# Attention of a four-layer graph network: weighted values by quarters of the queries, one order for every step

## The chip, the cores and the metric

The kernel runs on one core of one Trainium2 chip. The metric is the device time of one execution in microseconds (us). Three runs of the kernel before took 13,794.12, 13,808.5 and 13,815.49 us; the median is 13,808.5 us.

## The reference

Sixteen graphs of 1024 nodes with 64 features go through four layers. Each layer adds its result to its input and normalises. The change lies in layer 1, attention with 8 heads, which for each graph computes:

```
qkv   = x @ W_qkv.T                       # 8 heads of 64
attn  = (q @ k.T) / 8                     # per head, 1024 x 1024
attn  = g0 * attn + g1 * adj              # g0, g1 = exp(x @ W_gamma.T + b), per query node
out   = softmax(attn) @ v                 # per head, 1024 x 64
x     = layernorm(x + concat(out) @ W_proj.T + b_proj)
```

Layer 0 is a normalised graph convolution. Layer 2 takes quantiles of every feature over each node's neighbours, which the kernel finds from a sort of the features (`sort`) and a search over words of bits (`quantiles`). Layer 3 is a second graph convolution. All of them are left as they are, except for one buffer count in the sort.

## The kernel before

Graphs go in pairs. A loop of nine rounds does, in round p, layer 0 for pair p, then the attention of pair p with the sort of pair p-1 beside it, then the quantiles of pair p-1; layers 2 and 3 of a pair end in the round after. So there are eight stages of attention, each with both graphs of a pair, and a ninth sort that has no attention beside it.

One attention stage has 64 steps: 2 graphs x 4 pairs of heads (`hp`) x 2 halves of the queries (`nh`) x 4 blocks of 128 queries (`k4`). I call four steps with the same `nh` a half. A step has three pieces of work on TensorE, and this document uses short names for them:

- **Scores** (`scores`, L509): query times key for two heads, 128 queries x 1024 keys each, into two PSUM tiles called `banks` of two banks each; there are two such tiles, so four banks. VectorE then adds the adjacency and finds the row's extreme in one custom instruction per head (L516), which also frees the PSUM tile, and ScalarE takes the exponential (L518) with the row sum.
- **Transposes** (`transposes`, L529): the 2 x 8 blocks of the exponentials are transposed by TensorE, four into each of four PSUM tiles called `bank` (one bank each). ScalarE copies each of the four into the SBUF tile `pT` (L531). The pool `ps1` holds just four such `bank` tiles, and everything else that TensorE writes in the attention, projections (L488), values (L500), weighted values (L537) and output heads (L552), takes its tiles from the same four.
- **Weighted values** (`weighted`, L537): once per half, after its fourth step, 32 matmul instructions of 512 columns (8 blocks of keys x 2 heads x 2 passes for float32) sum into one `bank` tile `po`, which ScalarE copies into `o` (L540).

The order of TensorE's instructions in a stage is written out by hand: `in_sequence` gives a function `then` that ties every matmul to the one before it. A step issues the scores of the *next* step, then its own transposes. In the fourth step of a half the scores of the step after next are issued too, ahead of the weighted values. Projections of the next pair of heads follow the transposes in the steps (nh, k4) = (0, 2) and (1, 0). Values of a graph are made in its first four steps; the output heads of graph 0 in the first four steps of graph 1.

The order on VectorE and ScalarE is not written by hand. The tile framework lays each engine's queue out when the kernel is built, from its own estimate of when operands are ready, with the order of the program as priority. The sort's VectorE instructions (L1082) are emitted in step 58 (`BESIDE`) and so have low priority and fill gaps; `PACE` ties each swap of its second part to a score instruction that it may not overtake: 3, 9, 3 and 2 swaps for four steps in turn, the 9 falling on a step with weighted values. Its masks go to DRAM and come back through SP's queue, in tiles of which there are five.

Of the kernel before, what the change touches and what calls it, by code (L numbers as in the profile page):

```python
# [3 lines left out]

# [9 lines left out]
F32 = mybir.dt.float32  # L14
F16 = mybir.dt.float16
# [10 lines left out]
P = 128  # L26
N = 1024
C = 64
H = 8
NB = N // P  # L30
# [18 lines left out]
BESIDE = 58  # L49
AHEAD = (10, 12, 15)  # L50
STEPS = 55
PACE = (3, 9, 3, 2)
BN_EPS = 1e-5
LN_EPS = 1e-5

# [55 lines left out]
def gnn_kernel(ctx: ExitStack, tc: tile.TileContext, a: dict, out: bass.AP):  # L111
    nc = tc.nc
# [99 lines left out]
    def bank(shape, dtype=F32):  # L212
        return ps1.tile(shape, dtype, name="bank")
# [30 lines left out]
    HALF = [slice(0, C), slice(C, P)]  # L244
# [226 lines left out]
    def attention(nat, ip, graphs, wqkv, x2, beside):  # L471
# [3 lines left out]
        pace = []  # L475
        with (tc.tile_pool(name="att", bufs=2, reuse_waits="tile") as att,
# [3 lines left out]
            then = in_sequence()  # L480
# [12 lines left out]
            def values(gr, k):  # L493

                if k == 0:
                    gr.v = att1.tile([P, NB, H * C], F32, name="v")
                    gr.o = [att1.tile([P, N], F32, name=f"o{hp}") for hp in range(H // 2)]
                ps = [bank([P, H * C]) for f in range(2)]
                for f in range(2):
                    then(nc.tensor.matmul(ps[f], gr.xT[HALF[f], k * P:(k + 1) * P], wqkv[HALF[f], 2 * H * C:],  # L500
                                          start=True, stop=True))
                for f in range(2):
                    nc.scalar.copy(gr.v[:, 4 * f + k, :], ps[f])
# [17 lines left out]
                pace.append(last)  # L521
                return exps

            def transposes(exps, pT, k4):
                for h in range(2):
                    for mh in range(2):
                        ps = bank([P, 4, P])
                        for m in range(4):
                            then(nc.tensor.transpose(  # L529
                                ps[:, m, :], exps[h][:, (4 * mh + m) * P:(4 * mh + m + 1) * P], ident))  # L530
                        nc.scalar.copy(pT[h][mh][:, :, k4 * P:(k4 + 1) * P], ps)  # L531

            def weighted(gr, hp, nh, pT):
                po = bank([P, 512])
                for m in range(NB):
                    for h in range(2):
                        then(nc.tensor.matmul(po[HALF[h]], gr.v[:, m, (2 * hp + h) * C:(2 * hp + h + 1) * C],  # L537
                                              pT[h][m // 4][:, m % 4, :], start=(m == 0),
                                              stop=(m == NB - 1), tile_position=(0, h * C)))
                nc.scalar.copy(gr.o[hp][:, nh * 512:(nh + 1) * 512], po)  # L540

            def heads(gr, k):

                if k == 0:
                    nc.vector.reciprocal(gr.sm, gr.sm)
                smv = gr.sm.rearrange("p (f k) (q h) -> p h k f q", f=2, h=2)
                t = att1.tile([P, 2, 2, 4, C], F32, name="t_pr")
                pr = [bank([P, 2, 4, C]) for h in range(2)]
                for f in range(2):
                    for hp in range(H // 2):  # L550
                        for h in range(2):
                            then(nc.tensor.matmul(pr[h][:, f, hp, :],  # L552
                                                  gr.o[hp][HALF[h], (4 * f + k) * P:(4 * f + k + 1) * P],
                                                  wp[HALF[h], hp, :], start=True, stop=True))
                for h in range(2):
                    nc.vector.tensor_tensor(t[:, :, h], pr[h],
                                            smv[:, h, k, :, :, None].to_broadcast([P, 2, 4, C]), ALU.mult)
                x = gr.xg[:, k]
                nc.vector.tensor_reduce(x, t.rearrange("p f h q c -> p f c (h q)"), AX.X, ALU.add)
                nc.vector.tensor_tensor(x, x, bp_r[:, None, :].to_broadcast([P, 2, C]), ALU.add)  # L560
                nc.vector.tensor_tensor(x, x, gr.x1[:, k], ALU.add)
                if k == 0:
                    gr.norm = norm_tiles()
                norm_stats(gr.norm, gr.xg, [k])
                if k == 3:
                    norm_apply(gr.norm, by_half(x2)[:, :, :, gr.bb, :], gr.xg)
# [10 lines left out]
            def scores_of(st):  # L577
                if st < len(steps) and st not in exps:
                    gr, hp, nh, k4 = steps[st]
                    exps[st] = scores(gr, hp, 4 * nh + k4)  # L580

            scores_of(0)
            for st, (gr, hp, nh, k4) in enumerate(steps):
                if k4 == 0:
                    pT = [[att1.tile([P, 4, 512], F32, name="pT", bufs=4) for mh in range(2)] for h in range(2)]
                scores_of(st + 1)
                transposes(exps.pop(st), pT, k4)
                if k4 == 3:
                    scores_of(st + 2)
                at = 8 * hp + 4 * nh + k4  # L590
                if at < 4:
                    if gr is g1:
                        heads(g0, at)
                    values(gr, at)
                if st == BESIDE:
                    beside(pace)
                if st in AHEAD:
                    (keys_of, gates, queries_of)[AHEAD.index(st)](g1, att1, then)
                if gr is g0 and hp == H // 2 - 1:

                    k = 4 * nh + k4
                    g1.adj[k] = nat.tile([P, N], F32, name=f"adj{k}")
                    (nc.sync if k % 2 else nc.scalar).dma_start(
                        g1.adj[k], adj2d[ds((2 * ip + 1) * N + k * P, P), :])
                    gated(g1, k)
                if (nh, k4) in ((0, 2), (1, 0)):
                    if hp + 1 < H // 2:
                        project(gr, hp + 1, nh)
                    elif gr is g0:
                        project(g1, 0, nh)  # L610
                if k4 == 3:
                    weighted(gr, hp, nh, pT)
            for k in range(4):
                heads(g1, k)
            nc.gpsimd.dma_start(x2_d[ds(ip * P, P)], x2)
# [457 lines left out]
    def sort(keys, pool, key, pace, rk, u_w, b_w):  # L1073

        v = nc.vector

        behind = chain([None] * (3 * STEPS), (p for p, n in zip(pace, cycle(PACE)) for _ in range(n)))

        def swap(*args):
            i = v.tensor_tensor(*args)  # L1082
            p = next(behind, None)
            if p is not None:
                tc.add_manual_dep(i.ins, p.ins.name, in_order, reason="pace of the sort")


        steps = [(size, h) for p in range(1, 11) for size in (2 ** p,)
                 for h in [0] + [size >> s for s in range(2, p + 1)]]

        def pair(x, size, h):
            if h:
                r = x.rearrange("p (n two h) -> p n two h", two=2, h=h)
                return r[:, :, 0, :], r[:, :, 1, :]
            r = x.rearrange("p (n two h) -> p n two h", two=2, h=size // 2)
            return r[:, :, 0, :], r[:, :, 1, ::-1]

        def shaped(x, size, h):
            return x.rearrange("p (n h) -> p n h", h=h or size // 2)

        assert len(steps) == STEPS
        for i, (size, h) in enumerate(steps):
            new = keys.tile([P, N], F32, name="key", bufs=2)
            lo, hi = pair(key, size, h)
            nlo, nhi = pair(new, size, h)
            mask = keys.tile([P, N // 2], F16, name="mask", bufs=5)
            swap(shaped(mask, size, h), lo, hi, ALU.is_gt)
            nc.sync.dma_start(masks_d[:, i, :], mask)
            swap(nlo, lo, hi, ALU.min)
            swap(nhi, lo, hi, ALU.max)  # L1110
            key = new

        rank = pool.tile([P, N], F16, name="rank")
        nc.sync.dma_start(rank, a["c_iota"])
        d = pool.tile([P, N // 2], F16, name="d")
        for i, (size, h) in reversed(list(enumerate(steps))):
            lo, hi = pair(rank, size, h)
            mask = keys.tile([P, N // 2], F16, name="mask", bufs=5)
            nc.sync.dma_start(mask, masks_d[:, i, :])
            ds = shaped(d, size, h)  # L1120
            swap(ds, hi, lo, ALU.subtract)
            swap(ds, ds, shaped(mask, size, h), ALU.mult)
            swap(lo, lo, ds, ALU.add)
            swap(hi, hi, ds, ALU.subtract)
        words_of(pool, rank, rk, u_w, b_w)
        return key
# [110 lines left out]
```

## Time and profile before

The profiled execution took 13,812.89 us, 4.4 us more than the median of the three; its span, from the first to the last instruction in the profile, is 13,811.1 us. All numbers below are from this execution.

| What | us |
|---|---|
| TensorE busy, whole span | 12,369.8 (90%) |
| VectorE busy, whole span | 10,477.1 (76%) |
| ScalarE busy, whole span | 7,462.0 (54%) |
| Eight attention stages, first score to last weighted value, summed | 3,678.3 |
| One typical stage (5903.3 to 6362.0) | 458.7 |
| TensorE, ScalarE, VectorE busy in that stage | 437.8, 312.9, 276.4 |
| Granted TensorE clock in that stage, share of full | 0.97 |

A matmul's time in the profile is modelled and matmuls overlap in the array, so "busy" doesn't mean that the array is at its limit. What a group of matmuls really takes is read from the start of its first instruction to the start of the next group. In the timeline, "x16" after an instruction means that so many were merged into one row, and the brackets give the idle time of the engine before it and what ended that wait. In the chain, each row is the piece of time that the last instruction of the window had to wait for, followed backwards.

### The profile page before, as it was taken

How to read it: one execution, taken by the hardware profiler on the slowest of the kernel's cores; microseconds unless marked ns; L12 is line 12 of the kernel's file. 1: busy time of each engine (PE TensorE's matmuls, PEld its weight loads, DVE VectorE, ACT ScalarE, POOL GpSimd, SP SyncE). 2: the span in 40 equal slices, each digit the busy share in tenths (PEclk: the TensorE clock that was granted, in tenths of full speed). 3: DMA queues.
4: the chain of work that ended last, by engine and by line, in shares of the span. 5: the costliest groups of instructions: out<-in, count | busy, mean ns of one | idle time of the engine just before them, and what ended most of it. 6: DMA issues, size and time to landing. Idle time of an engine off the chain costs nothing.

```text
span 13811.1 us, 207433 instructions
## 1 busy us (share of the span) xinstructions
PE 12369.8 (90%) x81455; PEld 5244.9 (38%) x81536; DVE 10477.1 (76%) x18187; ACT 7462.0 (54%) x13548; POOL 635.5 (5%) x948
## 2 busy tenths in 40 slices
PE   7889998899979899798997989979899798993998
PEld 3544333443325433254333533335333353331332
DVE  3486887668876688766987678866788667887895
ACT  5666554555546555365553655536555465551553
POOL 0000000000000000000000000000000001000000
PEclk9999998999989999899998999989999899996999
DMA  2120002100031000310003100031000300002001
GB/s 76 34 92 21 4 6 94 63 17 4 5 104 53 16 5 5 119 40 14 5 5 128 32 13 6 5 130 30 14 5 5 131 29 14 9 8 88 4 5 43
DMA packets 356342, 510.35 MB, mean 37 GB/s; under 512 B 124448, under 2 KB 279584, under 8 KB 353312
## 3 DMA queue, kind: packets, MB, share of 16 engines
q1 hardware_dynamic: 288656, 371.94, 8.4%
q10 hardware_dynamic: 34192, 87.14, 2.0%
q0 software_dynamic: 32512, 38.00, 1.0%
q8 instruction: 638, 10.45, 0.3%
q14 instruction: 344, 2.82, 0.1%
HBM read 380.32 MB, written 116.59 MB: 36 GB/s over the span
## 4 chain that ended last, share of the span: by engine, by line
PE 68%; DVE 14%; ACT 6%; DMA 4%; issue 2%; SPq 0%; ACTq 0%; DVEq 0%
PE bank L815 33%; PE acc L815 9%; PE bank L537 6%; PE banks L509 6%; PE bank L529 4%; PE wps L815 4%; ACT s L518 3%; DVE m L847 2%; DMA at<-in_adjT 2%; ACT pT L531 1%; PE bank L392 1%; DVE key L1082 1%; PE banks L369 1%; PE bank L488 1%; PE bank L824 1%
## 5 line engine op out<-in xcount | busy, mean ns | idle before, releaser
L847 DVE TENSOR_TENSOR m<-V,oh 128x3072 bf16<-128x3072 bf16 x1536 | 2639.0, 1752 | 312.3 <-PE wps L815 286.4
L815 PE MATMUL bank<-ndT,E 128*128 128x512 fp8e4 x11904 | 2752.1, 381 | 7.1
L877 ACT ACTIVATE vals<-bank 128x512 f32<-128x512 f32 x3072 | 1592.2, 602 | 1401.5 <-PE bank L815 1399.9
L516 DVE CUSTOM_DVE_ANT_0 s<-banks,adj 128x1024 f32<-128x1024 f32 x1024 | 1214.1, 1222 | 1286.4 <-PE banks L509 1143.0
L825 ACT ACTIVATE V<-bank 128x512 uint16<-128x512 f32 x1536 | 911.8, 597 | 1745.3 <-PE bank L815 1644.6
L815 PEld LDWEIGHTS <-E 128*128 128x128 bf16 x11904 | 1116.6, 98 | 1790.1 <-issue 551.4
L839 ACT CAST oh<-bank 128x512 f16<-128x512 f32 x3072 | 1577.7, 601 | 297.1 <-PE bank L815 296.9
L815 PE MATMUL bank<-oh,bd 128*128 128x512 f16 x6144 | 1481.7, 385 | 0.0
L518 ACT ACTIVATE s<-s,mx 128x1024 f32<-128x1024 f32 x1024 | 1186.7, 1163 | 509.6 <-DVE mx L516 508.7
L509 PE MATMUL banks<-kT,qT 64*128 64x512 f32 x4096 | 1251.9, 636 | 47.2 <-ACT kT L491 28.4
L830 DVE TENSOR_TENSOR lt<-V,lim 128x2048 bf16<-128x2048 uint16 x768 | 934.0, 1216 | 224.1 <-PE bank L815 222.9
L531 ACT COPY pT<-bank 128x512 f32<-128x512 f32 x2048 | 1080.2, 598 | 32.2 <-PE bank L529 25.4
L529 PEld LDWEIGHTS bank<-ident,s 128*128 128x128 f32 x8192 | 891.6, 142 | 437.1 <-issue 233.3
L529 PE MATMUL bank<-ident,s 128*128 128x128 f32 x8192 | 1031.6, 279 | 18.2 <-ACT pT L531 16.2
L537 PE MATMUL bank<-pT,v 128*64 128x512 f32 x4096 | 985.0, 596 | 0.1
L815 PEld LDWEIGHTS <-bd 128*128 128x128 f16 x6144 | 542.4, 98 | 891.7 <-issue 357.1
L815 PE MATMUL bank<-lt,dif 128*128 128x512 bf16 x3072 | 814.3, 382 | 50.3 <-DVE lt L830 29.7
L815 PE MATMUL acc<-vals,bonesf 128*32 128x512 f32 x6144 | 849.4, 603 | 0.0
L815 PE MATMUL wps<-m,tonesb 128*32 128x512 bf16 x9216 | 643.2, 383 | 76.7 <-DVE m L847 76.7
L815 PE MATMUL bank<-r,pen 32*128 32x512 f16 x6144 | 488.7, 385 | 240.4 <-DVE r L734 226.4
L509 PEld LDWEIGHTS banks<-kT,qT 64*128 64x128 f32 x4096 | 521.0, 194 | 470.1 <-issue 295.9
L815 PE MATMUL acc<-oh,base 128*32 128x512 f16 x9216 | 642.3, 385 | 0.0
(247 smaller groups left out, 13110.8 us busy)
## 6 DMA issues: line engine op xcount, KB each, us to landing
at<-in_adjT SPq DMA_DIRECT2D x256, 512.0 KB, 5.4
masks_d<-mask SPq DMA_DIRECT2D x440, 128.0 KB, 1.7
mask<-masks_d SPq DMA_DIRECT2D x440, 128.0 KB, 2.1
adj<-in_adj SPq DMA_DIRECT2D x96, 512.0 KB, 5.9
ad<-in_adj ACTq DMA_DIRECT2D x64, 512.0 KB, 6.7
agg_d<-vals POOLq DMA_DIRECT2D x96, 256.0 KB, 2.3
agg<-agg_d ACTq DMA_DIRECT2D x16, 1536.0 KB, 7.8
nd_d<-nd SPq DMA_DIRECT2D x128, 128.0 KB, 1.9
```

Source lines behind the costliest of these rows:

```text
L509: then(nc.tensor.matmul(ss[h][:, hf * 512:(hf + 1) * 512], gr.qk[hp, 0][HALF[h], k * P:(k + 1) * P], gr.qk[hp, 1][HALF[h], hf * 512:(hf + ...
L516: last = nc.vector.tensor_tensor_reduce(s, ss[h], gr.adj[k], -1.0, 3.0e38, ALU.add, ALU.min, mx)
L518: nc.scalar.activation(s, s, AF.Exp, bias=mx, scale=-1.0, accum_out=gr.sm[:, k, 2 * hp + h:2 * hp + h + 1])
L529: then(nc.tensor.transpose(ps[:, m, :], exps[h][:, (4 * mh + m) * P:(4 * mh + m + 1) * P], ident))
L531: nc.scalar.copy(pT[h][mh][:, :, k4 * P:(k4 + 1) * P], ps)
L537: then(nc.tensor.matmul(po[HALF[h]], gr.v[:, m, (2 * hp + h) * C:(2 * hp + h + 1) * C], pT[h][m // 4][:, m % 4, :], start=(m == 0), stop=( ...
L815: then(nc.tensor.matmul(*args, **kw))
L825: nc.scalar.activation(gr.V[g][:, w, cols], ps, AF.Copy, bias=OFF)
L830: nc.vector.tensor_tensor(u.lt, gr.V[g][:, None, 0, :].to_broadcast([P, 2, N]), gr.lim[q], ALU.is_lt)
L839: nc.scalar.copy(oh[:, kk, cols], ps)
L847: nc.vector.tensor_tensor(u.m[kk], gr.V[g].bitcast(BF), u.oh[s][:, kk, None, :].to_broadcast([P, NW, N]), ALU.mult)
L877: nc.scalar.activation(vals[t], ys[t], AF.Relu)
```

## The change

- The transposed exponentials `pT` are kept by quarters of the queries: tiles of 256 columns instead of 512, eight of them instead of four (the same memory).
- `weighted` works on one quarter (two steps). It is a generator with two parts: the first four blocks of keys, then the last four and the copy into `o`. A quarter's parts are issued in the two steps that follow it, each after that step's transposes. The tile `po` stays in use from the first part to the end of the second.
- Scores of the step after next are no longer issued early: every step has scores of the next step, its own transposes, one part of weighted values.
- Of the four copies out of PSUM after the transposes, the first goes to VectorE.
- Values are made after step 1 (three blocks) and in step 2 (one), and the output heads of graph 0 in steps 2 to 5 of graph 1; so `o0` has two buffers.
- `PACE` is a constant 4 swaps for each step; the sort's mask tiles are four instead of five.

```diff
-PACE = (3, 9, 3, 2)
+PACE = 4
...
-                    gr.o = [att1.tile([P, N], F32, name=f"o{hp}") for hp in range(H // 2)]
+                    gr.o = [att1.tile([P, N], F32, name=f"o{hp}", bufs=1 if hp else 2) for hp in range(H // 2)]
...
-            def transposes(exps, pT, k4):
+            def transposes(exps, pT, k2):
...
-                        nc.scalar.copy(pT[h][mh][:, :, k4 * P:(k4 + 1) * P], ps)
-
-            def weighted(gr, hp, nh, pT):
-                po = bank([P, 512])
-                for m in range(NB):
-                    for h in range(2):
-                        then(nc.tensor.matmul(po[HALF[h]], gr.v[:, m, (2 * hp + h) * C:(2 * hp + h + 1) * C],
-                                              pT[h][m // 4][:, m % 4, :], start=(m == 0),
-                                              stop=(m == NB - 1), tile_position=(0, h * C)))
-                nc.scalar.copy(gr.o[hp][:, nh * 512:(nh + 1) * 512], po)
+                        dst = pT[h][mh][:, :, k2 * P:(k2 + 1) * P]
+                        if h or mh:
+                            nc.scalar.copy(dst, ps)
+                        else:
+                            nc.vector.tensor_copy(dst, ps)
+
+            def weighted(gr, hp, q, pT):
+
+                po = bank([P, 512])[:, 0:256]
+                for mh in range(2):
+                    for m in range(4):
+                        for h in range(2):
+                            then(nc.tensor.matmul(po[HALF[h]], gr.v[:, 4 * mh + m, (2 * hp + h) * C:(2 * hp + h + 1) * C],
+                                                  pT[h][mh][:, m, :], start=(mh == 0 and m == 0),
+                                                  stop=(mh == 1 and m == 3), tile_position=(0, h * C)))
+                    if mh == 0:
+                        yield
+                nc.scalar.copy(gr.o[hp][:, q * 256:(q + 1) * 256], po)
...
+            parts = iter(())
             for st, (gr, hp, nh, k4) in enumerate(steps):
-                if k4 == 0:
-                    pT = [[att1.tile([P, 4, 512], F32, name="pT", bufs=4) for mh in range(2)] for h in range(2)]
+                at = 8 * hp + 4 * nh + k4
+                if k4 % 2 == 0:
+                    pT = [[att1.tile([P, 4, 256], F32, name="pT", bufs=8) for mh in range(2)] for h in range(2)]
                 scores_of(st + 1)
-                transposes(exps.pop(st), pT, k4)
-                if k4 == 3:
-                    scores_of(st + 2)
-                at = 8 * hp + 4 * nh + k4
-                if at < 4:
-                    if gr is g1:
-                        heads(g0, at)
-                    values(gr, at)
+                if at == 2:
+                    values(gr, 3)
+                transposes(exps.pop(st), pT, k4 % 2)
+
+                next(parts, None)
+                if at == 0:
+                    for _ in parts:
+                        pass
+                if k4 % 2:
+                    for _ in parts:
+                        pass
+                    parts = weighted(gr, hp, 2 * nh + k4 // 2, pT)
+                if at == 1:
+                    for k in range(3):
+                        values(gr, k)
+                if gr is g1 and 2 <= at < 6:
+                    heads(g0, at - 2)
...
-                if k4 == 3:
-                    weighted(gr, hp, nh, pT)
+            for _ in parts:
+                pass
...
-        behind = chain([None] * (3 * STEPS), (p for p, n in zip(pace, cycle(PACE)) for _ in range(n)))
+        behind = chain([None] * (3 * STEPS), (p for p in pace for _ in range(PACE)))
...
-            mask = keys.tile([P, N // 2], F16, name="mask", bufs=5)
+            mask = keys.tile([P, N // 2], F16, name="mask", bufs=4)
```

(The last edit is made in two places.)

More of the change, by code (lines that the diff above doesn't have):

```diff
@@ L1 @@
 from contextlib import ExitStack, contextmanager
-from itertools import chain, cycle, islice
+from itertools import chain, islice
 from types import SimpleNamespace
@@ L1117, in sort @@
             lo, hi = pair(rank, size, h)
-            mask = keys.tile([P, N // 2], F16, name="mask", bufs=5)
+            mask = keys.tile([P, N // 2], F16, name="mask", bufs=4)
             nc.sync.dma_start(mask, masks_d[:, i, :])
```

## The prediction

> **What bounds the kernel now.** I read the page's busy times first: TensorE is busy for 90% of the span, so a stage is worth what its TensorE order loses. Then I read the chain of waits inside one regular half of the queries, from one weighted product to the next (start, length, what):
>
> ```profile
> 4351.52 7.71 PE bank L537 x32
> 4359.24 1.90 PE bank L529 x16
> 4361.14 1.06 PE bank L488 x4
> 4362.19 1.77 PE banks L509 x8
> ...
> 4365.32 1.24 ACT s L518 x2
> 4366.56 0.47 ACT pT L531
> 4367.03 1.14 ACT s L518 x2
> 4368.18 1.45 ACT pT L531 x3
> 4369.63 1.14 ACT s L518 x2
> 4370.77 0.48 ACT pT L531
> 4371.24 1.14 ACT s L518 x2
> 4372.38 0.49 ACT pT L531
> 4372.91 1.63 PE bank L529 x12
> 4374.55 2.29 PE banks L509 x8
> 4376.83 7.86 PE bank L537 x32
> ```
>
> The half takes 25.3 us. TensorE sets the time around the weighted product; ScalarE sets 7.6 us in the middle, where a step costs it 4.2 us (two exponentials at 1.14, four copies at 0.48) against TensorE's 3.7 (scores 1.82, transposes 1.90). During the 7.8 us of the product ScalarE has nothing to do. Over several halves the product starts at 4504.04, 4556.67 and 4609.27 us in the timeline, so a half is 26.3 us on average. Third, the timeline of a step in which TensorE needs a further PSUM tile right after its transposes (start, length, instruction, idle before it):
>
> ```profile
> 4340.36 1.97 PE L529 MATMUL bank<-ident,s 128*128 128x128 f32 x16
> ...
> 4341.46 1.18 ACT L518 ACTIVATE s<-s,mx 128x1024 f32<-128x1024 f32 x1
> ...
> 4342.60 0.60 ACT L531 COPY pT<-bank 128x512 f32<-128x512 f32 x1
> 4343.07 1.18 ACT L518 ACTIVATE s<-s,mx 128x1024 f32<-128x1024 f32 x1
> ...
> 4343.26 1.12 PE L488 MATMUL bank<-xgT,wqkv 64*128 64x512 f32 x2 [0.93 <-ACT pT L531]
> ...
> 4344.21 1.58 ACT L531 COPY pT<-bank 128x512 f32<-128x512 f32 x3
> ```
>
> The transposes fill all four `bank` tiles. The projection (L488) then waits for the first copy, which stands behind an exponential in ScalarE's queue: it starts 2.90 us after the transposes began instead of 1.90, and its other half waits for the second copy. Today only projections, values and heads meet this.
>
> [...]
>
> **The change part by part.** T is the start of a step's transposes.
>
> *Weighted values.* Today a half has one product of 7.02 us at best and 7.8 typically, since it starts on copies not yet made. In pairs of instructions at 0.429 us this is 16 pairs. Half the columns give 0.216 us a pair, eight pairs a part, and 0.1 for the change of group (0.52 from the last pair to the transposes, against 0.429): 1.83 us a part, four parts a half, 7.3 us. The product itself is no dearer. Weight loads double (137 ns each, two a pair, overlapped by 66 ns: 0.20 us against 0.216) and just fit; if each went alone, 0.274 a pair, it would be +0.46 us a part. I take 0.
>
> *Order.* Without other waits a step is scores 1.82, transposes 1.90, part 1.83 = 5.55 us; four with a projection of 0.96 are 23.2 us against 26.3. That is what the change could bring.
>
> *The fifth bank.* It doesn't get it. `po` lives from the first part (even step) to the end of the second (odd step). Even step: four transposed tiles and then `po`. Odd step: `po` is held, so the fourth group of transposes has no bank. Both need the first copy of the same step to have landed; call that time T + x. Scores end at T, and VectorE starts at T + 0.21 (4364.05 against 4363.84), its two score instructions at a pitch of 1.15 end the first two slots at T + 2.51, and the first exponential starts at T + 1.48. The copy moved to VectorE is emitted after both score instructions and they are ready first, so I place it third: 2.51 + 0.66 + 0.04 gives x = 3.2. ScalarE's first remaining copy comes no sooner: in the step at 4365 the exponential starts first although the bank was full, after idling, and over all 392 steps with fresh scores I counted 370 with an exponential ahead of the first copy, landing at 2.8 to 3.2. Behind one exponential it lands at 1.48 + 1.15 + 0.56 = 3.2 as well, behind two at 4.3. Bounds for x: 1.72, copied ahead of any exponential, and 4.3.
>
> *Sum.* Even step: x + 1.83 + 1.82 = 6.85. Odd: x + 0.53 (the last four transposes) + 1.83 + 1.82 = 7.38. A half: 2 x 6.85 + 2 x 7.38 + 0.96 = 29.4, or 4x + 16.6. Against 26.3 it is +3.1 us; 128 halves give +398.
>
> *Cover lost.* The early scores gave VectorE and ScalarE a step of work under the long product. That cover goes; what is late next is VectorE's pair of score instructions, with the copy behind them and TensorE's next group behind that. Queued behind the waiting matmul are the part and the next scores, for which VectorE waits in turn: the loop closes.
>
> *The rest.* No DMA issue moves to another step; adjacency loads and mask loads keep their places. ScalarE loses a copy of 0.5 a step and gains half-size `o` copies: nothing, since x doesn't hang on its load. VectorE per step: 2.4 + 0.66 + four swaps at 0.46 = 4.9 of 7.1 us, swaps in the gap after the copy: nothing; were they ahead of it, x would grow by 0.46 each. The sort's second part ends in step 55 instead of 52, still 60 us before the stage ends. Four masks on SP's queue, one used per step, loaded in 2.1 us: nothing; in its first part, beside layer 0, waits for masks are 40 us in total today and might double, at most +40. Values and heads: the zone of graph 0's heads costs 48.1 us for its half today, 21.8 over a plain one; spread out it has the same matmuls (values 4 x 0.95, heads 4 x 1.83) and 4 x 2.7 us of VectorE work ahead of the next scores' reduction, about 22: no difference. End of a stage: the last product is a quarter instead of a half after the last transposes, some -2 us, -16 in all.
>
> Sum: 398 - 16 = +382 us on the profiled execution's 13,812.9 (span 13,811.1): 14,195. It stood 4.4 us above the median, so **14,190 us**, +2.8%.
>
> **The rivals.**
> 1. *ScalarE empties a bank before the first exponential* (faster). It is idle by then, and the second tile is full at T + 1.1 (eight transposes at 0.109, then 0.2). Then x = 1.72, even steps wait for nothing (1.90): 2 x 1.90 + 2 x 1.72 + 16.6 = 23.9 a half, -2.4 x 128 - 16 = -327: 13,480. For it: 14 steps of today do so (first copy landed by T + 1.6), and the queue is laid out anew. Against it: the 370. It decides from x below 2.42, where 4x + 16.6 is 26.3.
> 2. *VectorE's copy between the two score instructions*: x = 1.36 + 0.6 + 0.04 = 2.0, a half 24.6, 13,580. Against it: both heads' scores end together, before any transpose.
> 3. *Weight loads don't overlap* at 256 columns: +0.46 x 512 parts = +236 on my sum, 14,430. For it: 0.20 of 0.216 us; against it, transposes load 128 columns every 0.109 us today.
> 4. *Nothing to see*: x near 2.42 by a mixture of orders, 13,810.
>
> **How the numbers follow.** A measurement of this kernel can tell about 0.2%, 28 us, from no change. Chances: my forecast 0.66, rival 3 0.08, rival 1 0.15, rival 2 0.05, rival 4 0.06; so slower 0.74, same 0.06, faster 0.20. The forecast's own range is x from 2.9 to 3.45 with the 40 us for masks: 14,040 to 14,360. To hold 8 in 10, the range takes in rival 4, the near edge of rival 2 and the near edge of rival 3: 13,600 to 14,400.
>
> **What would show it.** Right: about 500 us in a stage; TensorE's waits before L537's first matmul in even steps and before the fourth group of transposes in odd ones, ended by VectorE's (or the first ScalarE) copy, of 1.3 and 1.9 us; VectorE with a new copy row, x512 at about 0.66; L537 with 8192 matmuls at 0.108 us each in a part. Wrong: a ScalarE copy ahead of the exponentials, parts that start 1.90 us after T, or stages under 455 us.

## The result and the profile after

The changed kernel takes 14,304.2 us (median of four runs, 14,294.9 to 14,313.4) against 13,803.6 us before (the three runs above and a fourth): ratio 1.0362, 95% interval 1.0344 to 1.038, so 3.6% slower, inside the predicted range and above the predicted 14,190. Its profiled execution took 14,309.2 us with a span of 14,307.4, which is 496.3 us over the span before. The eight stages of attention sum to 4,170.1 us against 3,678.3. That is +491.8, so practically the whole loss lies in the attention. TensorE's granted clock over the span is 0.942 in both; in the single stages of attention it lies between 0.95 and 0.99 in both, so the clock doesn't explain the loss.

From the page of each kernel, the engines' shares of the chain that ended last, and groups of the attention (busy, mean ns of one | idle time before them and what ended most of it). First before:

```profile
PE 68%; DVE 14%; ACT 6%; DMA 4%; issue 2%; SPq 0%; ACTq 0%; DVEq 0%
...
L518 ACT ACTIVATE s<-s,mx 128x1024 f32<-128x1024 f32 x1024 | 1186.7, 1163 | 509.6 <-DVE mx L516 508.7
...
L529 PE MATMUL bank<-ident,s 128*128 128x128 f32 x8192 | 1031.6, 279 | 18.2 <-ACT pT L531 16.2
L537 PE MATMUL bank<-pT,v 128*64 128x512 f32 x4096 | 985.0, 596 | 0.1
```

Then after:

```profile
PE 58%; DVE 15%; issue 11%; ACT 7%; DMA 3%; POOL 0%; SPq 0%; DVEq 0%; ACTq 0%; POOLq 0%
...
L516 DVE CUSTOM_DVE_ANT_0 s<-banks,adj 128x1024 f32<-128x1024 f32 x1024 | 1215.1, 1222 | 1495.6 <-PE banks L509 1490.4
...
L518 ACT ACTIVATE s<-s,mx 128x1024 f32<-128x1024 f32 x1024 | 1176.7, 1149 | 1453.7 <-DVE mx L516 1451.9
...
L529 PE MATMUL bank<-ident,s 128*128 128x128 f32 x8192 | 1081.1, 281 | 415.6 <-ACT pT L533 383.8
L543 PE MATMUL bank<-pT,v 128*64 128x256 f32 x8192 | 1031.4, 397 | 328.5 <-ACT pT L533 270.6
```

TensorE's share of the chain was 68% and is 58%; "issue" was 2% and is 11%. The transposes (L529) had 18.2 us of waits before, and have 415.6. The weighted values (0.1 before, at L537) have 328.5. Both rows name the same releaser, ScalarE's copy of transposed exponentials (L533). ScalarE (L518) is not the cause by its load: its exponentials wait 1,453.7 us for VectorE's extreme, where they waited 509.6.

The chain of waits through one half, from one part of weighted values to the corresponding part of the next half (6276.19 to 6306.37, 30.2 us), is the counterpart of the chain of before in the prediction:

```profile
6274.42 1.24 ACT s L518 x2
6275.66 0.48 ACT pT L533
6276.14 0.04 issue
6276.19 1.95 PE bank L543 x16
6278.13 1.97 PE banks L509 x8
...
6281.46 1.24 ACT s L518 x2
6282.70 0.48 ACT pT L533
...
6283.22 0.66 PE bank L529 x4
6283.88 1.88 PE bank L543 x16
6285.76 1.97 PE banks L509 x8
...
6305.84 0.48 ACT pT L533
6306.32 0.04 issue
6306.37 0.43 PE bank L543
```

In every one of the four steps there is a stretch of the same form: the first exponential, one copy, and only then does TensorE go on. Before, the chain had ScalarE pieces only in the middle of a half. Now TensorE stands still once in each step. The timeline of an even and an odd step shows why (start, length, instruction, idle before it):

```profile
6272.94 1.97 PE L529 MATMUL bank<-ident,s 128*128 128x128 f32 x16
...
6274.42 1.15 ACT L518 ACTIVATE s<-s,mx 128x1024 f32<-128x1024 f32 x1 [2.70 <-DVE mx L516]
...
6275.45 0.69 DVE L535 COPY pT<-bank 128x512 f32<-128x512 f32 x1
...
6275.57 0.56 ACT L533 COPY pT<-bank 128x512 f32<-128x512 f32 x1
...
6276.19 1.95 PE L543 MATMUL bank<-pT,v 128*64 128x256 f32 x16 [1.28 <-ACT pT L533]
...
6279.98 1.53 PE L529 MATMUL bank<-ident,s 128*128 128x128 f32 x12
...
6281.46 1.15 ACT L518 ACTIVATE s<-s,mx 128x1024 f32<-128x1024 f32 x1 [3.23 <-DVE mx L516]
...
6282.49 0.69 DVE L535 COPY pT<-bank 128x512 f32<-128x512 f32 x1
...
6282.61 0.56 ACT L533 COPY pT<-bank 128x512 f32<-128x512 f32 x1
...
6283.22 0.66 PE L529 MATMUL bank<-ident,s 128*128 128x128 f32 x4 [1.71 <-ACT pT L533]
...
6283.81 1.95 PE L543 MATMUL bank<-pT,v 128*64 128x256 f32 x16
```

Even step: the sixteen transposes fill the four `bank` tiles, and the part needs a fifth. The part starts at T + 3.25 (T = 6272.94). Odd step: `po` is held, so only twelve transposes find a tile. The last four start at T + 3.24 (T = 6279.98). Both wait for the first copy of their own step. VectorE's copy (L535) ends at 6276.14 and ScalarE's first (L533) at 6276.13. The first stands behind two score instructions, the second behind one exponential. They land at the same time, so which of the two tiles TensorE is given can make little difference here. Over the whole kernel most steps are like these two: the part starts at T + 3.2 to 3.3 in 205 of 248 even steps, and at T + 3.8 to 3.9 (the late transposes included) in 194 of 240 odd ones.

Summed up by groups on TensorE in one stage (from the start of a group to the start of the next, waits for tiles included), the transposes grew from 138.8 to 227.4 us, the scores shrank from 151.6 to 132.0, weighted values went from 122.5 to 124.9, and projections, values and heads from 42 to 32. The sum is +60 us in a stage of 458.7. So scores and the small groups got about 30 us a stage shorter, and the transposes, whose figure holds both waits for a tile, 89 us longer.

### The profile page after: what moved, and what is told of

Same layout as the page of the kernel before. It is cut to its first block, busy times and chain, and to the rows that moved or that the text cites. A ratio compares the mean times of both kernels' runs of the same rounds, so it can differ in the third digit from the quotient of the medians.

```text
span 14307.4 us, 215539 instructions
## 1 busy us (share of the span) xinstructions
PE 12252.9 (86%) x85632; PEld 5281.9 (37%) x85632; DVE 10755.3 (75%) x18699; ACT 7246.7 (51%) x13164; POOL 626.8 (4%) x948
## 4 chain that ended last, share of the span: by engine, by line
PE 58%; DVE 15%; issue 11%; ACT 7%; DMA 3%; POOL 0%; SPq 0%; DVEq 0%; ACTq 0%; POOLq 0%
PE bank L834 29%; PE acc L834 7%; PE bank L543 6%; PE banks L509 5%; ACT s L518 4%; PE wps L834 3%; DVE m L866 2%; DMA at<-in_adjT 2%; PE bank L392 1%; ACT pT L533 1%; DVE key L1101 1%; PE bank L529 1%; DVE s L516 1%; PE banks L369 1%; PE bank L843 1%
## 5 line engine op out<-in xcount | busy, mean ns | idle before, releaser
L518 ACT ACTIVATE s<-s,mx 128x1024 f32<-128x1024 f32 x1024 | 1176.7, 1149 | 1453.7 <-DVE mx L516 1451.9
L529 PE MATMUL bank<-ident,s 128*128 128x128 f32 x8192 | 1081.1, 281 | 415.6 <-ACT pT L533 383.8
L543 PE MATMUL bank<-pT,v 128*64 128x256 f32 x8192 | 1031.4, 397 | 328.5 <-ACT pT L533 270.6
L529 PEld LDWEIGHTS bank<-ident,s 128*128 128x128 f32 x8192 | 894.8, 142 | 872.4 <-ACT pT L533 443.8
L509 PE MATMUL banks<-kT,qT 64*128 64x512 f32 x4096 | 1077.8, 624 | 55.6 <-ACT kT L491 28.6
L533 ACT COPY pT<-bank 128x512 f32<-128x512 f32 x1536 | 826.3, 576 | 29.0 <-PE bank L529 28.9
L543 PEld LDWEIGHTS bank<-pT,v 128*64 128x64 f32 x8192 | 559.5, 140 | 669.5 <-ACT pT L533 320.7
```

Source lines behind the costliest of these rows:

```text
L509: then(nc.tensor.matmul(ss[h][:, hf * 512:(hf + 1) * 512], gr.qk[hp, 0][HALF[h], k * P:(k + 1) * P], gr.qk[hp, 1][HALF[h], hf * 512:(hf + ...
L518: nc.scalar.activation(s, s, AF.Exp, bias=mx, scale=-1.0, accum_out=gr.sm[:, k, 2 * hp + h:2 * hp + h + 1])
L529: then(nc.tensor.transpose(ps[:, m, :], exps[h][:, (4 * mh + m) * P:(4 * mh + m + 1) * P], ident))
L533: nc.scalar.copy(dst, ps)
L543: then(nc.tensor.matmul(po[HALF[h]], gr.v[:, 4 * mh + m, (2 * hp + h) * C:(2 * hp + h + 1) * C], pT[h][mh][:, m, :], start=(mh == 0 and m ...
```

## The experiments

Theory: the fifth `bank` tile is not there, the wait lasts until the first copy lands, and that copy lands late because of its place in a queue. Rivals: VectorE's copy as such is too slow; the loss of the early scores; the sort's new pace; the weighted values dearer in quarters. In the kernels with a changed order the transposes are at L536, the weighted values near L550 and the exponentials at L520.

**Is it the place of the copy?** The first copy on ScalarE is put ahead of both exponentials. For that, a step's score instructions and exponentials are emitted after its transposes, and each exponential is tied to follow the copy:

```diff
-                exps = []
-                for h in range(2):
+                def reduced(copy=None):
+                    exps = []
+                    for h in range(2):
...
+                        if copy is not None:
+                            tc.add_manual_dep(e.ins, copy.ins.name, in_order, reason="copy first")
...
-                transposes(exps.pop(st), pT, k4 % 2)
+                first = transposes(exps.pop(st), pT, k4 % 2)
+                if st + 1 in exps:
+                    exps[st + 1] = exps[st + 1](first)
```

> The changed kernel, with TensorE's order untouched; on ScalarE the first of the three copies out of PSUM must stand ahead of both exponentials of the next step's scores. Theory (the fifth PSUM tile): the first copy now lands 1.8 us after the transposes begin instead of 3.2, so the part of an even step waits for nothing (1.90 after the transposes begin instead of 3.24) and the fourth group of transposes in an odd step for about 0.45 us instead of 1.9. A half goes from 30.2 to about 24.7 us and the kernel from 14,304 to 13,600, below the kernel before. Rivals (VectorE's new copy, the narrower products, or the lost early scores make it slow): all three are as in the changed kernel, so it stays at 14,300.

Measured: 13,620.7 us, ratio to the kernel before 0.9868 (0.9853 to 0.9882). The timeline of an odd step of this kernel:

```profile
5953.23 1.53 PE L536 MATMUL bank<-ident,s 128*128 128x128 f32 x12
...
5954.36 1.07 ACT L540 COPY pT<-bank 128x512 f32<-128x512 f32 x2 [1.87 <-PE bank L536]
...
5955.00 0.66 PE L536 MATMUL bank<-ident,s 128*128 128x128 f32 x4 [0.24 <-ACT pT L540]
5955.32 1.16 ACT L520 ACTIVATE s<-s,mx 128x1024 f32<-128x1024 f32 x1
```

The copy starts when its tile is full (T + 1.13), and the last four transposes start at T + 1.77 instead of 3.24. Of the 248 even steps with a part, 209 don't wait at all. 684 us go with the order of one queue and the later emission that it needs; the two are separated further down.

**Is it VectorE's copy?** All four copies are put on ScalarE, with no other edit:

```diff
-                        if h or mh:
-                            nc.scalar.copy(dst, ps)
-                        else:
-                            nc.vector.tensor_copy(dst, ps)
+                        nc.scalar.copy(dst, ps)
```

> The changed kernel with all four copies on ScalarE. Theory (the fifth PSUM tile): ScalarE's first copy stands behind one exponential as before and lands 3.2 us after the transposes begin, when VectorE's does too; within 40 us of the changed kernel, 14,260 to 14,350. Rival (VectorE's copy is what TensorE waits for, or it crowds VectorE): the wait goes, 13,950 or less.

Measured: 14,286.4 us, ratio 1.035 (1.0335 to 1.0365), 18 us below the changed kernel. The move to VectorE didn't make the loss and didn't ease it.

**Does it matter what is waited for?** Each part is put ahead of the transposes, so that `po` takes its tile before they fill all four:

```diff
-                transposes(exps.pop(st), pT, k4 % 2)
-
                 next(parts, None)
...
+                transposes(exps.pop(st), pT, k4 % 2)
```

> The changed kernel with the part of the weighted values issued ahead of the step's transposes instead of after them. Theory (the fifth PSUM tile): the sum tile is taken while all four tiles are free, and while the part runs, VectorE and ScalarE come to the first copy; only the fourth group of transposes waits, 0.1 us or so. A step is 1.88 + 1.9 + 1.92 = 5.75 us, a half 23.9 with a projection, 6.3 less than the changed kernel's 30.2 and 2.4 less than before: 13,500. Rivals (VectorE's copy, narrower products, lost early scores): nothing of these is altered, 14,300.

Measured: 13,880.6 us, 1.0057 (1.0042 to 1.0072). The direction was right, but it misses the expectation by 380 us. The timeline shows what I had left out:

```profile
6088.78 1.53 PE L529 MATMUL bank<-ident,s 128*128 128x128 f32 x12
...
6089.41 0.42 DVE L1101 TENSOR_TENSOR d<-rank 128x512 f16<-128x512 f16 x1
...
6089.86 0.43 DVE L1101 TENSOR_TENSOR d<-d,mask 128x512 f16<-128x512 f16 x1
6090.21 0.68 DVE L535 COPY pT<-bank 128x512 f32<-128x512 f32 x1
...
6090.95 0.66 PE L529 MATMUL bank<-ident,s 128*128 128x128 f32 x4 [0.64 <-DVE pT L535]
```

Now the score instructions are over when the transposes begin, VectorE is free, and two of the sort's swaps (L1101) get ahead of the copy in its queue. The copy starts at T + 1.43 though its tile was full at about T + 0.65 (an estimate: four transposes at 0.109, and the 0.21 us from the end of scores to VectorE's start in the prediction), and the last four transposes start at T + 2.17. Over the whole kernel the matmuls of the transposes wait 211.4 us for VectorE's copy. Stage 0, which has no sort beside it, takes 438 us, most of the others 470. To take the swaps out of it, the first copy goes to ScalarE, between the two exponentials, and the last to VectorE; the emission is as in the first experiment:

```diff
-                        if h or mh:
+                        if not (h and mh):
...
+                        if copy is not None and h:
+                            tc.add_manual_dep(e.ins, copy.ins.name, in_order, reason="copy first")
```

> The part ahead of the transposes as in e3, with the first copy on ScalarE and held between the two exponentials, and the last of the four on VectorE instead of the first. In e3 the fourth group of transposes waited 0.85 us or more for VectorE's copy, which the sort's swaps had got ahead of; a ScalarE copy behind one exponential is not in their reach and lands 1.35 us after the transposes begin. Theory (the fifth tile waits for whichever copy is first): no wait is left, the transposes take 1.90 us in every step, a step 5.7 and a half 23.7: 13,480, 400 below e3. Rival (e3 lost its gain because a part ahead of the transposes waits for its own operands or because VectorE has too much work): as e3, 13,880.

Measured: 13,590.0 us, 0.9854 (0.984 to 0.9869), 290 us below the run before it. The swaps aren't the whole difference: stage 0, which has none, goes from 438 to 422 us as well. Transposes now take 1.90 to 2.17 us and a regular half about 24.4 us instead of the 23.7 expected: 0.7 x 128 = 90 of the 110 us missing. Part of it is the scores that follow a projection, which take 2.19 instead of 1.81.

**Does the split in two parts matter?** A whole quarter is issued in the even step, none in the odd one:

```diff
-                next(parts, None)
-                if at == 0:
-                    for _ in parts:
-                        pass
+                for _ in parts:
+                    pass
```

> The changed kernel with both parts of a quarter in the even step, so that the sum tile isn't held across an odd step. Theory (the fifth PSUM tile): the odd step's transposes take 1.90 us instead of 3.83 and that step is held by VectorE's turn from scores to scores, some 4.4 us; the even step still waits 1.34 us for the first copy and holds 3.6 us of products, 8.8 us. A half is 27.2 us instead of 30.2: 13,930. Rivals (narrower products, VectorE's copy): the same products and copies, 14,300.

Measured: 13,995.3 us, 1.0141 (1.0124 to 1.0158). With no `po` held over an odd step its transposes take 1.90, while the even step still waits (3.17). One wait of two is gone, and 309 us with it, 65 less than expected. The wait goes and stays with the fifth tile, step by step.

**What is the early score worth?** In the kernel before, only the early issue of the scores is taken out:

```diff
-                if k4 == 3:
-                    scores_of(st + 2)
```

> The kernel before with one thing of the change alone: scores of the step after next are not issued ahead of the weighted values. Theory (the early scores are the cover of the long product, and the product's own tile is a fifth one): the product waits 1.3 us for the first copy, and the four steps of a half have to be fed after it instead of three, some 1 to 2.5 us more in a half: 14,000 to 14,300. Rival (the early scores bought nothing, the change's loss is all in holding the sum tile over two steps): 13,800 to 13,850.

Measured: 14,446.7 us, 1.0473 (1.0456 to 1.0491), outside the expectation. That is 652 us over the kernel before on the same chip (13,794.9), or 5.1 a half, more than the whole change lost. Not all of it need be lost cover: the granted clock of the stages is 0.91 to 0.94 here, against 0.95 to 0.98 before. Summed over the eight stages, the share of full speed that wasn't granted is 305 us against 118, so by this estimate the lower clock accounts for at most 188 of the 652; the runs don't separate the two. The timeline around the weighted values:

```profile
6275.89 1.07 PE L537 MATMUL bank<-pT,v 128*64 128x512 f32 x2 [0.92 <-ACT pT L531]
...
6277.99 7.08 PE L537 MATMUL bank<-pT,v 128*64 128x512 f32 x30 [1.03 <-ACT pT L531]
...
6287.13 1.22 DVE L516 CUSTOM_DVE_ANT_0 s<-banks,adj 128x1024 f32<-128x1024 f32 x1 [11.18 <-PE banks L509]
```

The product now takes 9.1 us: it waits 0.92 for its own tile and 1.03 for the operands' copies, both behind exponentials. VectorE's score instructions have nothing to work on meanwhile: the next one comes 11.18 us after VectorE's last work. The changed kernel has no early scores either and lost less, so what else it changes took back a part.

**The sort's pace and buffers alone**, in the kernel before:

```diff
-PACE = (3, 9, 3, 2)
+PACE = 4
...
-            mask = keys.tile([P, N // 2], F16, name="mask", bufs=5)
+            mask = keys.tile([P, N // 2], F16, name="mask", bufs=4)
```

> The kernel before with the edits in the sort alone: four swaps for each step instead of 3, 9, 3 and 2, and four mask tiles instead of five. Theory: they cost nothing that shows, 13,780 to 13,840. Rival (an even pace puts swaps in front of score reductions, which the 9 in the long product's step avoided, or masks are waited for): 13,900 or more.

Measured: 13,815.2 us, 1.0014 (1.0006 to 1.0022): 20 us, too little to explain a loss of 500.

**The best order.** The kernel of the first experiment with the copies exchanged: first on ScalarE, ahead of the exponentials, and last on VectorE:

```diff
-                        if h or mh:
+                        if not (h and mh):
```

> e1 (a ScalarE copy ahead of both exponentials) with the first of the four copies as that one, so that it lands 1.3 us after the transposes begin instead of 1.75, and with the last copy on VectorE. Theory (the fifth tile): the 0.45 us that the fourth group waits in each odd step of e1 goes, 64 x 0.46 x 4 = 118 us: 13,500. Rival (what is left in e1's odd steps is not that wait): 13,620 as e1.

Measured: 13,461.8 us, 0.9761 (0.9747 to 0.9776), below both kernels. A step of it:

```profile
5904.28 1.97 PE L536 MATMUL bank<-ident,s 128*128 128x128 f32 x16
...
5904.97 1.56 ACT L540 COPY pT<-bank 128x512 f32<-128x512 f32 x3 [1.63 <-PE bank L536]
...
5906.17 1.95 PE L552 MATMUL bank<-pT,v 128*64 128x256 f32 x16
5906.40 1.17 ACT L520 ACTIVATE s<-s,mx 128x1024 f32<-128x1024 f32 x1
```

The first copy starts at T + 0.69 and has landed by T + 1.3, so the part follows the sixteen transposes at T + 1.89 with no wait. The chain of waits through these steps holds TensorE pieces only, 5.7 us a step. ScalarE's exponential comes at T + 2.12 and is late for nobody. Does VectorE's share matter here? All four copies on ScalarE:

```diff
-                        if not (h and mh):
-                            c = nc.scalar.copy(dst, ps)
-                            first = first or c
-                        else:
-                            nc.vector.tensor_copy(dst, ps)
+                        c = nc.scalar.copy(dst, ps)
+                        first = first or c
```

> The kernel with the quarters and the first copy on ScalarE ahead of the exponentials, the last one on VectorE, with one edit: all four copies on ScalarE. Theory (only the landing of the first copy frees the tile for the fourth transposes, and that is unchanged; ScalarE has some 4.4 us of work in a step of 5.7): 13,440 to 13,520. Rival (the last copy, now behind two exponentials on ScalarE, comes too late for its part, or VectorE's share relieves ScalarE): 13,560 or more.

Measured: 13,457.6 us, 0.975 (0.9733 to 0.9766). The intervals overlap: which engine makes the fourth copy is no difference that these runs can tell.

**Is it the tie, or the changed place of emission?** From that kernel only the tie is taken away:

```diff
-                            tc.add_manual_dep(e.ins, copy.ins.name, in_order, reason="copy first")
+                            pass
```

> The kernel with the quarters and all four copies on ScalarE, where so far each step's exponentials were emitted after its transposes and tied behind the first copy. One edit: the tie is taken away, the place where they are emitted stays; ScalarE's queue then has one or both exponentials ahead of the copies again, TensorE's order is the same and VectorE's nearly so. Theory (the place of the copy in ScalarE's queue decides, not where things are emitted for VectorE): 14,200 to 14,500, transposes or parts waiting again, 3.2 us or more from the start of the transposes to the part. Rival (the gain came from the changed place of the score instructions): 13,440 to 13,600.

Measured: 14,206.1 us, 1.03 (1.0282 to 1.0317). TensorE's order is the same, instruction by instruction, and almost 750 us are back. What the place of emission does by itself is the rest: against the run with all copies on ScalarE and the old emission (14,286.4 us) it is some 80 us. An odd step:

```profile
6283.48 1.53 PE L536 MATMUL bank<-ident,s 128*128 128x128 f32 x12
...
6284.96 1.15 ACT L520 ACTIVATE s<-s,mx 128x1024 f32<-128x1024 f32 x1 [2.73 <-DVE mx L518]
...
6286.11 2.03 ACT L539 COPY pT<-bank 128x512 f32<-128x512 f32 x4
...
6286.73 0.66 PE L536 MATMUL bank<-ident,s 128*128 128x128 f32 x4 [1.71 <-ACT pT L539]
```

ScalarE idles for 2.73 us, the last 0.8 of them with a full tile (in the best order a copy starts 0.69 us after its transposes began; here T = 6283.48), and then an exponential goes ahead of all four copies. The last transposes start at T + 3.25, as in the changed kernel.

**And in the kernel before?** The same tie with the product by halves and the early scores kept:

```diff
-                        nc.scalar.copy(pT[h][mh][:, :, k4 * P:(k4 + 1) * P], ps)
+                        c = nc.scalar.copy(pT[h][mh][:, :, k4 * P:(k4 + 1) * P], ps)
+                        first = first or c
...
+                        if copy is not None:
+                            tc.add_manual_dep(e.ins, copy.ins.name, in_order, reason="copy first")
```

> The kernel before with one edit: the first copy of a step's weights (ScalarE, columns 0:2) is put ahead of the step's exponentials. Theory (the order of the copy matters where a group of matmuls waits for it; in the old kernel the weighted values of a half lie a whole half behind, so only the fourth transposes wait for a tile, and the middle of the half is bound by ScalarE and VectorE anyway): 13,690 to 13,800; the part to be won is the wait of the transposes with a projection ahead of them, 1.66 us at some 7 or 8 places of each stage, about 93 us. Rival (the order alone is the whole gain, the quarters of the queries bring nothing): 13,460 to 13,500 as with the quarters and this order.

Measured: 13,522.5 us, 0.9797 (0.9783 to 0.9812). My expectation was too small by far, and the rival nearly right: 273 us under the kernel before on the same chip, where the best version is 338 under it, so most of that gain comes with the order of ScalarE's queue. (The granted clock rises a little too, to between 0.97 and 0.99 in the stages; worked out as above, that can be at most 61 of the 273 us.) I had counted only the projections' waits. In one stage (458.7 us before, 423.1 now) the weighted values lose 10 us, the transposes 10, the scores 6, the heads 5, the projections 3 and the values 2. The product, which used to start on copies not yet made (7.8 us), starts at once and takes its 7.0:

```profile
6051.11 7.09 PE L546 MATMUL bank<-pT,v 128*64 128x512 f32 x32
...
6062.81 1.97 PE L536 MATMUL bank<-ident,s 128*128 128x128 f32 x16
...
6063.50 2.05 ACT L538 COPY pT<-bank 128x512 f32<-128x512 f32 x4 [1.24 <-PE bank L536]
...
6065.41 1.18 ACT L520 ACTIVATE s<-s,mx 128x1024 f32<-128x1024 f32 x1
```

The copies (L538) run as four in a row from T + 0.69, and the exponential follows them. Without the early scores as well:

```diff
-                if k4 == 3:
-                    scores_of(st + 2)
-                    if st + 2 in exps:
-                        exps[st + 2] = exps[st + 2]()
```

> The kernel before with the first copy ahead of the exponentials, and in addition no early scores ahead of the weighted product. Without the order this removal cost 640 us, 5 us a half. Theory (it cost that much because the product waited for its own tile and for its operands' copies behind exponentials, and VectorE idled behind it; with the copies early the product starts at once and takes 7.0 us, and a half is 7.0 + 0.96 + 3.7 + 3 x 4.2 to 4.6, some 24.3 to 25.5 us): 13,480 to 13,640. Rival (the early scores cover 5 us a half in any order): 14,050 to 14,200.

Measured: 13,675.4 us, 0.9916 (0.9901 to 0.9931): 35 us above the expectation's upper end, and nowhere near the rival. The expectation took the product at 7.0 us; here it typically takes 7.44. The early scores are worth 153 us here, against some 640 (with its lower clock) where exponentials go first. Put together (medians in us; the runs are from several chips, on which the kernel before stood between 13,791 and 13,805; "copy first" has the later emission as well, and the row of quarters all other edits of the change):

| Weighted values | exponentials first | copy first |
|---|---|---|
| by halves, early scores (as before) | 13,803.6 | 13,522.5 |
| by halves, no early scores | 14,446.7 | 13,675.4 |
| by quarters, all copies on ScalarE | 14,286.4 | 13,457.6 |

From left to right the rows gain 281, 771 and 829 us. In the right column no two rows differ by more than 218 us, in the left one by up to 643: what an order of TensorE's work is worth depends on where the copy stands. Against halves without early scores, the quarters gain 160 and 218. Against the kernel before they lose 483 in the left column and gain 65 in the right one.

## Why the prediction was right, step by step

- **The fifth bank**: right. Both waits are where the text put them, 1.28 us before the part in even steps and 1.71 before the last transposes in odd ones (forecast 1.3 and 1.9). With a whole quarter in one step, the wait of the odd steps goes, as the count of live tiles says. That the pool could have held no fifth tile was not shown: no run tries it.
- **x = 3.2, the landing of the first copy**: measured 3.24. VectorE's copy did stand third, and ScalarE's landed at the same time. The reading behind it was rougher than it looks: the trace before has 384 steps that follow fresh scores, not 392; 370 do have an exponential ahead, but the first copy lands at T + 2.4 to 3.2 in most of them and near 4.0 in the 32 with two ahead. The sum's 0.66 for VectorE's copy had no row of the trace before behind it; the nearest one, a two-input operation on 128x512 in PSUM (L556), has a median of 0.683, which gives 3.23 in the same sum. The changed kernel's 512 copies (L535) take 0.686 (median; 0.656 to 0.693).
- **Weight loads in parts of 256 columns**: right that they fit. A part takes 1.88 us, where loads without overlap would, by the forecast's estimate, have given 2.29. In the timeline at 6276 the pairs of matmuls follow one another at 0.216 us, as forecast, while one instruction lasts 0.38, and the two loads of the next pair lie under the running ones. They take 0.14 us together (0.137 each, the second 0.007 behind the first), where the forecast had read 0.20.
- **The sum, +382 us**: the mechanism right, the size low by 114. A half takes 30.2 instead of 29.4 us. Terms: scores 1.92 instead of 1.82 where no projection stands ahead of them (3 x 0.10), parts 1.88 instead of 1.83 (4 x 0.05), x 3.24 (4 x 0.04), the last transposes 0.59 instead of 0.53 (2 x 0.06): 0.78 together, x 128 = 100 us. Three of the four are the change from one group of matmuls to the next, which I had read as smaller: the 1.82 for scores was read behind a projection, and the trace before has 1.92 as well where no projection stands ahead. (30.2 - 26.3) x 128 = 499 against the 496.3 measured. The 16 us for the ends of stages barely show.
- **The cover lost**: named as the reason why VectorE's score instructions come late, but not priced by itself. In the old kernel its loss costs 5.1 us a half, the lower clock included, and with the copy first 153 us in all, 1.2 a half. So it isn't a term of fixed size; how much of the changed kernel's 3.9 us a half is owed to it no run separates.
- **The sort, masks, values and heads at nothing**: right for pace and buffers (20 us). Spread out, values, heads and projections got 10 us a stage cheaper, which I had put at no difference.
- **The rivals**: the first, a copy ahead of the exponential, forecast 13,480. Made by hand it gives 13,620.7. Its x of 1.72 is measured as 1.77, the half's other terms are the 0.6 us dearer named above, and parts wait another 43.8 us for VectorE's copy. So the rival had the right price for an order that the layout of the queue didn't choose. The second (VectorE's copy between the score instructions) did not occur. The third is refuted by the 1.88, the fourth by the 496 us.

Left open: why the layout of ScalarE's queue prefers an exponential to a copy whose tile is full. The runs show that it does, and what it costs, not by which estimate.

## What to carry to other kernels

Before a step gets one more PSUM tile in flight, count the tiles that are live in it. Where the count exceeded the pool here, TensorE stood until the first eviction (a copy that empties a tile) had landed, 1.28 us before a part and 1.71 before the last transposes, and the place of that eviction in its engine's queue set the price. In these kernels an eviction that frees a tile for TensorE belonged ahead of long work that nobody waited for yet. Where the layout doesn't put it there, an explicit order does, and it is worth trying before any rearrangement of TensorE's own order: here it gained 2.0% with the old order, and turned the new one from 3.6% slower into 2.4% faster.

## What the runs showed that I had not expected

- The same order on TensorE is a loss or a gain by one tie in ScalarE's queue: by quarters 14,206.1 or 13,457.6 us, with no instruction of TensorE added, removed or moved.
- An engine with time to spare (VectorE, idle 2.10 us before the score instructions of the steps at 6087, 6093 and 6100 in the kernel with the part ahead) still delayed a copy by two swaps of 0.42 us, since low-priority work had been laid out ahead of it. Most stages with a sort took some 32 us longer than the one without, against 7 to 10 in the changed kernel.
- Two copies on two engines end within 0.01 us of one another, and the profile puts 383.8 us of the transposes' waits on TensorE down to ScalarE's and 13.2 to VectorE's. Without VectorE's copy the time fell by 18 us of 500. Whether moving either would help can't be read from such rows; only a kernel with another order told it.
